# A four-layer graph attention stack on one core: the order of work planned for pairs of graphs, with tiles placed by colouring

## The chip, the core and the metric

The kernel runs on one core of a Trainium2 chip. The metric is the device time of one execution in microseconds (us). Before the change the median of three runs is 3231.36 us (3228.59 to 3233.77). The engines are named as in the profile: PE (matrix products), PEld (loading of the stationary operand for PE), DVE (vector), ACT (scalar functions), POOL (general vector), SP (issues most of the DMAs). Each engine works through its own queue in order, and semaphores hold an instruction until what it needs is there.

## What is computed

128 independent graphs of 128 nodes with 512 features each pass through four attention layers. Each layer is followed by a residual sum and a layer norm. Cut to what matters:

```
# layer 0: one head, scores from x itself
a = softmax(where(adj + eye == 0, -inf, leaky(s_src[:,None] + s_dst[None,:] + b)))
x = layernorm(x + a @ x)
# layer 1: two nested layers, 4 heads of 256, then 1 head of 512; softmax over the sources
xl = x @ W1                       # 512 -> 1024, plus 8 score columns
h  = elu(attention(xl) + b1)
x  = layernorm(x + attention(h @ W2) + b2)      # 1024 -> 512, plus 2 score columns
# layer 2: 8 heads of 64
h  = x @ W                        # 512 -> 512, plus score columns
x  = layernorm(x + concat(attention_per_head(h)))
# layer 3: one head, scores from x, elu of the result
x  = layernorm(x + elu(attention(x)))
```

All of it is in float32. A matmul of float32 operands is two records of PE in the profile (the mask transpose is one).

## The kernel before

One graph is a list of some 180 operations, each with an engine, a cost, an `emit` function, and the tiles it reads and writes. The list is made by `graph` (L567), in three parts:

- `first` (L830): loads, masks, layer 0, the norm, and the turning of x for the first projection. `project` (L704, matmuls at L710, evictions at L717) then makes the first projection, four chunks of four matmuls of 258 columns.
- `second` (L864): attention with four heads; the attention product and the bias and elu (`block`, L896 on PE, L902 on ACT, L903 on DVE). The elu is made as min(exp(v), 1) and max with the sum in PSUM; it is written into a tile of its own beside the tile of exponentials.
- `third` (L911): attention of the nested second layer, norm (L681 to L699), the last projection (L710 with wha), eight heads in two groups of four (`heads`, L938 and L942), the norm, and layer 3 (wide attention products at L725).

`attend` (L637) is the common attention step: ACT's Prelu per head (L646), DVE's masking with a running minimum (L654), ACT's exponential per head (L663), DVE's reciprocal (L671). `turned` (L602) transposes in two steps: DVE turns blocks of 32 (L607), the tile is written to DRAM (scr, L612) and is read back in another order (L617 or L622). `spread` (L580) lays a column of scores over all partitions, also by way of DRAM (row, L592 and L596). Each graph issues 30 DMAs from SP's queue.

The second projection (1024 to 512) is made for two graphs at a time with a seven-product scheme of Strassen's kind (`halves`, L749): POOL makes four sums of the left operands (L780), PE seven products of four matmuls of 257 columns (L794) in four PSUM banks, and evictions go by ACT (L807) or by a DVE addition (L812). As the list is per graph, a pair's products are divided between the list of the odd graph and that of the next even one.

The order of work is set by a planner that runs while the program is built (`Pipeline`, L75). `plan` (L79) places one graph's operations on every engine in a period of 28 us, by costs and by delays between engines that stand in a table. `order` (L145) then runs the operations of all graphs as a list: each engine takes the ready operation that can start first, at most 20 us ahead of the oldest one that is not issued. It counts 4.5 us and a shared lane for a DMA. A tile is given a place when it is first written, and the place is the one that has been free longest:

```
                b.slot = free[b.tag].pop(0)[1]
```

The places of each kind are as many as the plan needs; PSUM has eight. The setup of the weights (L305 to L555) is in the same list, with times of its own.

Of the kernel before, what the change touches and what calls it, by code (L numbers as in the profile page):

```python
# [26 lines left out]

PERIOD = 28.0
LATENCY = {"PE": (0.0, 0.8), "DVE": (0.15, 1.44), "ACT": (0.1, 1.44), "POOL": (0.1, 1.44), "SP": (7.06, 7.06)}
FLOW = {"PE": (0.0, 0.6), "DVE": (0.15, 0.8), "ACT": (0.1, 0.8), "POOL": (0.1, 0.8), "SP": (4.5, 4.5)}
AHEAD = 20.0
URGENCY = 0.6
BANKS = 8

SEED, SPREAD = 989, 8.0


class Buf:


    def __init__(self, tag, shape, dtype=F32):
        self.tag, self.shape, self.dtype = tag, shape, dtype
        self.size = 1
        for d in shape[1:]:
            self.size *= d

        if dtype is F32 and shape[0] == P and self.size in (P, 4 * P, 8 * P) and not tag.startswith(("ps", "scr")):  # L50
            self.tag = f"w{self.size}"
        self.ap = self.slot = None

# [7 lines left out]
class Op:  # L61
    def __init__(self, engine, cost, emit, ins, outs, extra, uses=(), dma=0.0):
        self.dma = dma
        self.engine, self.cost, self.emit, self.extra = engine, cost, emit, extra
        self.wait = 0
        self.ins, self.outs = ins, outs
        self.uses = list(uses)
        self.bufs = list(dict.fromkeys([*ins, *outs, *uses]))

    def done(self, reader=None):  # L70
        own, other = LATENCY[self.engine]
        return self.cost + self.extra + (own if reader is self.engine else other)


class Pipeline:  # L75
    def __init__(self, make, n, place):
        self.make, self.n, self.place = make, n, place

    def plan(self, ops):  # L79


        before, after = [set() for _ in ops], [[] for _ in ops]
        last, readers = {}, {}
        for k, op in enumerate(ops):
            for b in op.ins:
                before[k].add(last[b])
            for b in op.outs:
                if b in last:
                    before[k].add(last[b])
                before[k].update(readers.get(b, ()))  # L90
            before[k].discard(k)
            for q in before[k]:
                after[q].append(k)
            for b in op.ins:
                readers.setdefault(b, set()).add(k)
            for b in op.outs:
                last[b], readers[b] = k, set()
        left = [0.0] * len(ops)
        for k in reversed(range(len(ops))):
            left[k] = ops[k].cost + max(  # L100
                (left[q] + ops[k].done(ops[q].engine) - ops[k].cost for q in after[k]), default=0.0
            )
        taken = {e: [] for e in LATENCY}
        times, ready, missing = [0.0] * len(ops), [0.0] * len(ops), [len(q) for q in before]
        waiting = [k for k in range(len(ops)) if not missing[k]]
        rng = random.Random(SEED)
        shift = [SPREAD * rng.random() for _ in ops]
        while waiting:
            k = min(waiting, key=lambda k: (ready[k] - URGENCY * left[k] + shift[k], k))
            waiting.remove(k)  # L110
            op, t = ops[k], ready[k]
            spans = taken[op.engine]
            while True:
                u = t % PERIOD
                clash = [
                    y + d - u for x, y in spans for d in (-PERIOD, 0.0, PERIOD)
                    if u < y + d - 1e-9 and x + d < u + op.cost - 1e-9
                ]
                if not clash:
                    break  # L120
                t += min(clash) + 1e-9
                assert t < ready[k] + 2 * PERIOD, "the period is too short"
            spans.append((t % PERIOD, t % PERIOD + op.cost))
            times[k] = t
            for q in after[k]:
                ready[q] = max(ready[q], t + op.done(ops[q].engine) + max(ops[q].wait, 0) * PERIOD)
                missing[q] -= 1
                if not missing[q]:
                    waiting.append(q)
        return times  # L130

    def run(self, setup):
        times, events = self.plan(self.make(None)), [(t, -1, k, op) for k, (t, op) in enumerate(setup)]
        for g in range(self.n):
            for k, op in enumerate(self.make(g)):
                if op is not None:
                    events.append((g * PERIOD + times[k], g, k, op))
        events.sort(key=lambda e: e[:3])
        for g, op in self.order(events):
            for b in op.outs:  # L140
                if b.ap is None and b.slot is not None:
                    b.ap = self.place(b, g)
            op.emit()

    def order(self, events):  # L145

        ops, n = [e[3] for e in events], len(events)
        ends, first, last, readers, open_uses = {}, {}, {}, {}, {}
        before, after = [0] * n, [[] for _ in ops]
        makes, coming = [[] for _ in ops], {}  # L150
        for i, op in enumerate(ops):
            need = {last[b] for b in op.ins + op.uses if b in last}
            for b in op.outs:
                need.update([last[b]] if b in last else [], readers.get(b, ()))
                if b not in first:
                    first[b] = events[i][0]
                    if b.tag != "const":
                        makes[i].append(b)
                        coming.setdefault(b.tag, []).append(i)
            need.discard(i)  # L160
            before[i] = len(need)
            for q in need:
                after[q].append(i)
            for b in op.ins + op.uses:
                readers.setdefault(b, []).append(i)
            for b in op.outs:
                last[b], readers[b] = i, []
            for b in op.bufs:
                open_uses[b] = open_uses.get(b, 0) + 1
                ends[b] = max(ends.get(b, 0.0), events[i][0] + op.done())  # L170

        free = {}
        for b, t in first.items():
            if b.tag != "const":
                places = free.setdefault(b.tag, [])
                s = next((s for s, e in enumerate(places) if e <= t), len(places))
                places[s : s + 1] = [ends[b]]
        assert len(free["ps"]) <= BANKS, "too few banks"
        free = {tag: [(0.0, s) for s in range(BANKS if tag == "ps" else len(p))] for tag, p in free.items()}
        ready, released, clock, lane = [0.0] * n, {}, {e: 0.0 for e in FLOW}, 0.0  # L180
        known = {e: [i for i in range(n) if not before[i] and ops[i].engine == e] for e in FLOW}
        issued, low, out = [False] * n, 0, []

        def start(i):
            t = max(clock[ops[i].engine], ready[i])
            for b in makes[i]:

                rank = 0
                for q in coming[b.tag]:
                    if q >= i or rank >= len(free[b.tag]):  # L190
                        break
                    rank += 1
                if rank >= len(free[b.tag]):
                    return None
                t = max(t, free[b.tag][rank][0])
            return t

        while len(out) < n:
            best = None
            for e, waiting in known.items():  # L200
                found = None
                for i in waiting:
                    if events[i][0] > events[low][0] + AHEAD and i != low:
                        break
                    t = start(i)
                    if t is not None and (found is None or t < found[0]):
                        found = (t, i)
                        if t <= clock[e]:
                            break
                if found and (best is None or found < best):  # L210
                    best = found
            t, i = best
            op = ops[i]
            known[op.engine].remove(i)
            issued[i] = True
# [6 lines left out]
            if op.engine == "POOL":  # L222
                other += op.extra
# [20 lines left out]
def tile_gat_stack(  # L244
# [86 lines left out]
    def spread_row(t, r, a):  # L331
# [5 lines left out]
        return b  # L337

# [700 lines left out]
```

## Time and profile before

| what | value |
|---|---|
| median of three runs | 3231.36 us |
| profiled execution: its span | 3258.4 us |
| instructions in it | 62058 |
| PE busy | 94% of the span |
| DVE, ACT, POOL busy | 85%, 75%, 58% |
| granted PE clock, mean | 0.976 |
| DMA | 606.08 MB, 186 GB/s |

The profiled execution is one execution of its own. Its time is its span, from the first to the last instruction of the program, and it is 27.0 us longer than the median of the runs.

The page first gives each engine's busy time and its share of the span. A strip of 40 digits then shows that share in tenths, slice by slice. Groups of instructions are named by line, engine, operation and tile, with the idle time of the engine before them and what ended it. Matmuls overlap, and their ends are modelled, so a PE that is shown busy may still lose time between two starts.

### The profile page before, as it was taken

How to read it: one execution, taken by the hardware profiler on the slowest of the kernel's cores; microseconds unless marked ns; L12 is line 12 of the kernel's file. 1: busy time of each engine (PE TensorE's matmuls, PEld its weight loads, DVE VectorE, ACT ScalarE, POOL GpSimd, SP SyncE). 2: the span in 40 equal slices, each digit the busy share in tenths (PEclk: the TensorE clock that was granted, in tenths of full speed). 3: DMA queues.
4: the chain of work that ended last, by engine and by line, in shares of the span. 5: the costliest groups of instructions: out<-in, count | busy, mean ns of one | idle time of the engine just before them, and what ended most of it. 6: DMA issues, size and time to landing. Idle time of an engine off the chain costs nothing. (4 is left out here: it accounts for less than half of the span.)

```text
span 3258.4 us, 62058 instructions
## 1 busy us (share of the span) xinstructions
PE 3066.8 (94%) x14822; PEld 2488.7 (76%) x14822; DVE 2779.0 (85%) x9833; ACT 2451.2 (75%) x8741; POOL 1895.1 (58%) x2347
## 2 busy tenths in 40 slices
PE   6899999999999999999999999999999999999984
PEld 4688887787777877877777778777787777878853
DVE  4779888888888988898888889889898898989875
ACT  2457787787777777787777877777877777778875
POOL 4655655665565655665555665565566556565533
PEclk7899999999999999999999999999999999999985
DMA  4358777877877877877778777877787787777875
GB/s 119 94 136 196 183 205 188 200 193 190 203 187 188 205 186 192 201 190 200 188 187 200 191 188 204 189 190 201 191 204 187 188 205 188 196 196 190 197 174 129
DMA packets 1657567, 606.08 MB, mean 186 GB/s; under 512 B 1311562, under 2 KB 1508170, under 8 KB 1657204
## 3 DMA queue, kind: packets, MB, share of 16 engines
q1 hardware_dynamic: 1655836, 598.97, 75.0%
q8 instruction: 120, 1.97, 0.2%
q14 instruction: 243, 1.99, 0.2%
q0 software_dynamic: 576, 2.10, 0.2%
q10 hardware_dynamic: 792, 1.06, 0.1%
HBM read 374.43 MB, written 227.48 MB: 185 GB/s over the span
## 5 line engine op out<-in xcount | busy, mean ns | idle before, releaser
L710 PE MATMUL ps<-w1s,w 128*128 128x258 f32 x4096 | 926.9, 384 | 48.5 <-DMA w<-scr 25.0
L710 PEld LDWEIGHTS ps<-w1s,w 128*128 128x128 f32 x4096 | 777.0, 191 | 186.3 <-DVE xl L812 39.5
L654 DVE CUSTOM_DVE_ANT_0 w<-w,w 128x128 f32<-128x128 f32 x1920 | 861.1, 544 | 65.6 <-ACT w L646 49.2
L794 PE MATMUL ps<-w2s,w 128*128 128x257 f32 x3584 | 849.0, 383 | 8.5 <-POOL w L780 8.4
L663 ACT ACTIVATE w<-w,nm 128x128 f32<-128x128 f32 x1920 | 748.0, 394 | 98.2 <-DVE nm L654 76.3
L794 PEld LDWEIGHTS ps<-w2s,w 128*128 128x128 f32 x3584 | 669.1, 191 | 188.8 <-issue 80.0
L646 ACT ACTIVATE w<-w,xl 128x128 f32<-128x128 f32 x1536 | 488.8, 389 | 279.9 <-DMA w<-row 259.1
L607 DVE STREAM_TRANSPOSE w<-w 128x512 f32<-128x512 f32 (+1 forms) x1024 | 551.5, 540 | 34.3 <-ACT w L663 13.3
L710 PE MATMUL ps<-wha,w 128*128 128x273 f32 x2048 | 502.3, 398 | 7.3 <-DMA w<-scr 6.9
L710 PEld LDWEIGHTS ps<-wha,w 128*128 128x128 f32 x2048 | 383.2, 192 | 87.4 <-DVE w L607 6.3
L699 ACT ACTIVATE w<-w,mr,rd 128x512 f32<-128x512 f32 x512 | 415.2, 811 | 33.9 <-POOL mr L692 33.0
L692 POOL TENSOR_SCALAR mr<-mv,rd 128x1 f32<-128x1 f32 x512 | 160.1, 313 | 409.4 <-ACT rd L686 201.8
L663 ACT ACTIVATION_READ_ACCUMULATOR w<-w,nm 128x1 f32 x1920 | 368.1, 192 | 0.0
L681 DVE BATCH_NORM_STATS2 st<-w 128x6 f32<-128x512 f32 x512 | 337.2, 668 | 5.4 <-POOL w L986 4.6
L881 POOL TENSOR_TENSOR xl<-xl,b1t 128x512 f32<-128x512 f32 x256 | 335.2, 1310 | 1.6
L938 PEld LDWEIGHTS ps<-xl,w 128*128 128x128 f32 x2048 | 274.3, 196 | 80.8 <-issue 24.4
L646 ACT ACTIVATE w<-w,sc 128x128 f32<-128x128 f32 x384 | 152.3, 397 | 227.6 <-DMA w<-row 226.6
L725 PE MATMUL ps<-w,w 128*128 128x512 f32 x512 | 277.4, 624 | 32.6 <-DMA w<-scr 31.6
L738 POOL TENSOR_SCALAR w<-adj 128x128 f32<-128x128 int32 x256 | 192.4, 752 | 188.2 <-DMA adj<-in_adj_dram 75.1
L717 ACT COPY xl<-ps 128x258 f32<-128x258 f32 (+1 forms) x768 | 273.2, 362 | 31.8 <-PE ps L710 31.3
L938 PE MATMUL ps<-xl,w 128*128 128x66 f32 x2048 | 265.2, 273 | 27.7 <-DMA w<-scr 14.4
L654 DVE DVE_READ_ACCUMULATOR2_ANT nm<- 128x1 f32 x1920 | 290.5, 151 | 0.0
(213 smaller groups left out, 4258.8 us busy)
## 6 DMA issues: line engine op xcount, KB each, us to landing
scr<-w SPq DMA_DIRECT2D x640, 256.0 KB
w<-scr SPq DMA_DIRECT2D x640, 256.0 KB
w<-row SPq DMA_DIRECT2D x128, 512.0 KB
w<-in_x_dram SPq DMA_DIRECT2D x128, 256.0 KB
w<-row SPq DMA_DIRECT2D x128, 256.0 KB
out_dram<-w SPq DMA_DIRECT2D x128, 256.0 KB
w<-row SPq DMA_DIRECT2D x384, 64.0 KB
scr<-w SPq DMA_DIRECT2D x384, 64.0 KB
```

The lines of the kernel that those rows point to most:

```text
L607: op("DVE", 0.12 + 0.133 * n, lambda: nc.vector.transpose(zb.ap.rearrange("p b h c -> p h b c"), src.ap.rearrange("p (h b c) -> p h b c", ...
L646: nc.scalar.activation(z.ap[:, h, :], db.ap[:, h0 + h, :], AF.Prelu, bias=src(h0 + h), alpha=SLOPE)
L654: nc.vector.tensor_tensor_reduce(out=zz.ap[:, h, :].rearrange("p (b a) -> p a b", b=4), in0=z.ap[:, h, :].rearrange("p (a b) -> p a b", b= ...
L663: nc.scalar.activation(zz.ap[:, h, :], zz.ap[:, h, :], AF.Exp, bias=nm.ap[:, h : h + 1], scale=-1.0, accum_out=rs.ap[:, h : h + 1],)
L681: op("DVE", 0.6, lambda: nc.vector.bn_stats(st.ap, y.ap), [y], [st])
L699: op("ACT", 0.7, lambda: nc.scalar.activation(y.ap, y.ap, AF.Identity, bias=mr.ap, scale=rd.ap), [y, rd, mr], [y])
L710: op("PE", w * 4 / 2400 + 0.006, lambda k=k: nc.tensor.matmul(px.ap[:, :w], lhsT=lhs.ap[:, k, :], rhs=wa(k, c), start=(k == 0), stop=(k == ...
L717: op("ACT", 0.06 + w / 1200, lambda: nc.scalar.copy(dst(), px.ap[:, :w]), [px], [t])
L725: op("PE", width * 4 / 2400, lambda: nc.tensor.matmul(pa.ap[:, :width] if len(xv.shape) == 2 else pa.ap.rearrange("p (s c) -> p s c", s=2) ...
L794: return lambda: nc.tensor.matmul(q[b].ap[:, :C2], lhsT=x()[:, k, :], rhs=w2s[:, slot, k, :], start=(fresh and k == 0), stop=(k == 3), ski ...
L881: op("POOL", 1.3, lambda nh=nh: nc.gpsimd.tensor_add(xl.ap[:, nh, : 2 * FH], xl.ap[:, nh, : 2 * FH], b1t[:, nh * 2 * FH : (nh + 1) * 2 * F ...
L938: op("PE", 0.225, lambda u=u, h=h: nc.tensor.matmul(pa.ap[:, u * CH : (u + 1) * CH], lhsT=pt.ap[:, u, :], rhs=xl3.ap[:, h * CH : (h + 1) * ...
```

## The change

The list is now made for a pair of graphs (`pair`), with one list of operations per pair and the two graphs' first parts half a period apart. Strassen's products stand in it as one unit. The planner is three functions: `needs` finds the dependences, `plan` places one pair in a period of 53 us, and `lay_out` runs all pairs as a list, at most 60 us ahead. An operation has a duration for each of its parts, as the profile shows them, and each engine a tail. A DMA takes 1.7 us to start, its time on a lane that all share, and 0.6 us to land, with at most eight under way. POOL and those DVE operations that are marked `port` exclude one another. Evictions into one tile are `joins`: they are not ordered among themselves. All matmuls of an accumulation are one operation. Places are given after the list run, by colouring: a tile takes, among the places that the run left free early enough, the one freed last.

```diff
-PERIOD = 28.0
-LATENCY = {"PE": (0.0, 0.8), "DVE": (0.15, 1.44), "ACT": (0.1, 1.44), "POOL": (0.1, 1.44), "SP": (7.06, 7.06)}
-FLOW = {"PE": (0.0, 0.6), "DVE": (0.15, 0.8), "ACT": (0.1, 0.8), "POOL": (0.1, 0.8), "SP": (4.5, 4.5)}
-AHEAD = 20.0
...
-SEED, SPREAD = 989, 8.0
+PERIOD, PACE, AHEAD = 53, 53, 60
+HOP = {'PE': 0.5, 'DVE': 0.5, 'ACT': 0.5, 'POOL': 0.5, 'SP': 1.0}
+URGENCY, SEED, SPREAD = 0.3, 87533, 16.0
+BANKS, PRODUCTS = 8, 2
...
+FLIGHT, LANDS = 1.7, 0.6
+LANES = 8
+SLACK = 1.0
...
+        if e == "POOL":
+            u = max(u, vector_until)
...
+            if op.port:
+                u = max(u, pool_until)
...
+        if e == "SP":
+            lane = max(lane, t + FLIGHT) + op.dma
+            got = [lane + LANDS]
...
+    for b in sorted({b: None for op in ops for b in op.bufs if b.tag != "const"}, key=lambda b: b.began):
+        places = free.setdefault(b.tag, [])
+        slack = 0.0 if b.tag in scarce else SLACK
+        fit = [s for s in range(len(places)) if places[s] + slack <= b.began]
+        b.slot = max(fit, key=lambda s: places[s]) if fit else len(places)
+        places[b.slot : b.slot + 1] = [b.until]
```

Strassen's scheme uses three banks. Bank pa holds four of the products one after another, adding up, and is evicted between them; the last one needs no addition on DVE:

```diff
+        product(pa, left[0][0], 0, True)
...
+        taken(pa, t1)
+        product(pc, left[0][1], 1, True)
+        added(pc, t1, 0, 0)
+        product(pa, s[1], 4, False)
+        product(pb, s[0], 3, True)
+        taken(pa, u2)
+        taken(pb, v)
+        product(pa, s[2], 5, False)
+        product(pb, s[3], 2, False)
+        added(pa, v, 1, 1)
+        added(pb, u2, 0, 1)
+        product(pa, left[1][1], 6, False)
+        copied(pa, wide, lambda: to(1, 0), joins=[out[1]])
```

The elu is made in place, and each half of its result is a tile of its own:

```diff
-                op("ACT", 0.6, lambda: nc.scalar.activation(half(e1), pa.ap, AF.Exp, bias=minus[:, 0:1]), [pa], [e1])
-                op("DVE", 0.65, lambda: nc.vector.scalar_tensor_tensor(
-                    out=half(hT), in0=half(e1), scalar=1.0, in1=pa.ap, op0=ALU.min, op1=ALU.max
-                ), [e1, pa], [hT])
+            op("ACT", 0.585, lambda pa=pa, whole=whole: nc.scalar.activation(whole(), pa.ap, AF.Exp, bias=minus[:, 0:1]), [pa], [hT[c]])
+            op("DVE", 0.585, lambda pa=pa, whole=whole: nc.vector.scalar_tensor_tensor(
+                out=whole(), in0=whole(), scalar=1.0, in1=pa.ap, op0=ALU.min, op1=ALU.max
+            ), [hT[c], pa], [hT[c]])
```

The setup's work for the second and the last projection is the same, and its times in the list are earlier (for the sums of the second projection's weights 50 to 71 instead of 89 to 109, for the last projection's columns 79 to 113 instead of 139 to 201). In the new program the first projection, the second and the last one share one matmul line (L702), the evictions are at L710, the attention products at L838 (first layer), L878 (heads) and L771 (wide), and Strassen's additions at L747.

## The prediction

> **What bounds the kernel now.** I read the page's first two parts, then the table of stretches, then who waited for whom in the even middle, 400 to 2900 us.
>
> ```profile
> PE 3066.8 (94%) x14822; PEld 2488.7 (76%) x14822; DVE 2779.0 (85%) x9833; ACT 2451.2 (75%) x8741; POOL 1895.1 (58%) x2347
> PE   6899999999999999999999999999999999999984
> PEclk7899999999999999999999999999999999999985
> ```
>
> PE is busy in nine slices of ten, and only the first and last slices are weak, in its share and in its granted clock. So there are three stages: fill, middle, drain.
>
> ```profile
> 58.00:134.00 76.00, 60.85 (x244) 47.00 (x244) 55.67 (x129) 34.60 (x111) 63.20 (x59) 0.81 0.39 98
> ...
> 400.00:2900.00 2500.00, 2413.65 (x11882) 1973.60 (x11882) 2201.57 (x7856) 1956.23 (x7025) 1495.68 (x1859) 1.00 0.79 194
> 2900.00:3069.00 169.00, 164.55 (x819) 136.09 (x818) 147.47 (x532) 135.72 (x489) 99.84 (x126) 1.00 0.80 197
> 3069.00:3259.00 190.00, 130.26 (x522) 96.26 (x521) 131.19 (x486) 131.13 (x452) 68.11 (x103) 0.75 0.65 155
> ```
>
> Columns: stretch, its length, then busy us of PE, PEld, DVE, ACT and POOL, granted clock, DMA share, GB/s. In the middle PE is busy 2413.65 of 2500 us. L896 has 1648 matmul records there and 16 in a graph, so 103 graphs pass: 24.27 us each, 0.84 us of it with PE idle. What PE must spend I take from starts in its timeline, from the start of a run to that of the next: first projection 6.96, first-layer attention 1.79, last projection 3.69, heads twice 0.83, wide attention products three times 0.86, second projection 14 x 0.44, mask transpose 0.14, in all 22.98 us. So 1.29 us of a graph is loss: 0.84 shows as idle, 0.45 is hidden between starts. No other engine is above 88% (DVE 2201.57 of 2500) and DMA is at 0.79: **PE bounds it**, and a reordering can win at most what PE loses.
>
> ```profile
> PE ps L710 <- DMA w<-scr: 22.9, 23, 1.7
> PE ps L725 <- DMA w<-scr: 14.7, 25, 1.3
> PE ps L850 <- DVE w L903: 13.7, 14, 1.9
> PE ps L710 <- DVE ri L671: 9.3, 9, 2.1
> ...
> PEld ps L710 <- DVE xl L812: 36.9, 29, 2.5
> ...
> PEld ps L725 <- ACT xl L717: 26.2, 46, 1.7
> ```
>
> Waits of matmuls and, below the dots, of weight loads in the middle: us in total, times, longest. 37.6 us of PE's 86 idle us is for data that comes by way of DRAM (w<-scr). The weight loads' waits on L812 and L717, which are evictions of PSUM, are waits for a bank: 1.27 and 0.57 us each.
>
> **The change, part by part.** It removes no matmul and no DMA. In the built programs PE has 7475 matmuls before and after, ACT 6820 instructions, POOL 2349, SP 3873 DMAs; DVE has 64 fewer. So the sum is about order and waits.
>
> *Three-bank Strassen.* One DVE addition in each pair of graphs becomes a plain ACT eviction (there were four of L807 and there are three and one of its kind now). 64 x 404 ns (L812) = 26 us of DVE go. DVE is idle 12% of the middle: nothing on the path. Bank pa now takes four products in a row; each needs the eviction of the one before. In the built order even the closest two of one bank have 1.88 us of other PE work between them (a product and a transpose), against L812's 0.40 us and an eviction's 0.36. I cost it at 0; if DVE comes late there, a wait is 1.27 us as for L812 today.
>
> *elu in place, the two halves of hT as separate buffers, evictions of one tile unordered among themselves.* Same instructions (L902, L903, L981, L982). Cost 0; their order on one queue was kept anyway. Matmuls of a chain issued together instead of singly: same start-to-start times expected, 0.
>
> *Setup.* The same loads and products; those of the second and last projection are due some 40 to 90 us earlier. They are POOL's (16 of 1.25 us from L472, 16 of 1.2 us from L504), and POOL is busy 63 of 76 us from 58 to 134 us. PE's work ahead of the first projection is 13.5 us against 15.3. I take 0, from -15 (the weak fill has 39 us of PE idle) to +10 (one mask late: PE's L850 once waited 9.0 us for L738).
>
> *Drain.* After the last matmul of the first projection 301 DVE operations are left in the old order and 242 in the new (SP 177 and 143), and 99.9 and 74.9 us of PE work. The drain lasts 190 us now. By operations left it would be 190 x 242/301 = 153, so -37; the 25.0 us of PE work now done earlier cost 25.0 x 24.27/22.98 = +26. Sum **-11**; between -37 (the moved work fits into idle time) and 0.
>
> *The list run.* Its own durations now agree with rows: a masked softmax step 0.226 (L654 starts 0.23 apart), wide transposes 0.61, an exponential 0.387 (0.29 and its accumulator read). It also gives each DMA a queue of eight and a time by size, holds POOL and some DVE operations apart, and gives small tiles more places (nm4 five for one, rs4 four for one). From 134 to 3069 us some 121 graphs' worth of time passes. Ends: none of the idle goes (0), or all of it (121 x 0.84 = -102). I take half, nearest to the share that is waits for DMA (37.6 of 86 us), the thing that the new durations describe better: 121 x 0.42 = **-51**.
>
> *Places by colouring, for the banks too.* The old order took the bank that had been free longest, the new one takes the one freed last. Counted in the built order with the durations above, the PE work between a bank's last matmul and its next tenant falls from a median of 7.4 us to 1.8; in 16% of the takings, five in a pair, it is under 1 us, where formerly none was under 2. An eviction needs 0.36 us (L717) and some hand-over. This adds waits on ACT and DVE behind which all of PE stands, and every engine behind PE. No row has such a wait at such a distance; the nearest is L725 on L717, 0.57 us each. Ends: never (0), or half of the five and a quarter of the eleven others under 2 us, 5.2 a pair: 64 x 5.2 x 0.57 = +190. I take one in two pairs, **+18**: the run itself knew each bank to be free at that time.
>
> Here the trace comes first: L725's 46 waits on L717 show that late evictions do stop PE. The Trainium skill, "Perfetto Trace Analysis", section "Matmuls", says that independent groups should rotate through different PSUM banks so that one's evacuation overlaps the next; it speaks against this colouring. It gives no price; by it the sum would take the upper end, 3231 - 62 + 190 = 3359, by the rarity of such waits in the rows it stays at 3187.
>
> Another row: POOL's one-column L692 waited 123.9 us for L654, which writes nothing it reads. The Trainium skill, "SBUF — State Buffer", section "SBUF: two separate sides", calls the port pair of DVE and GpSimd an exclusive lock held for a whole instruction. By the rule 15 masks of 0.23 us would lock POOL out 3.4 us a graph; the row has 123.9/103 = 1.2 us. POOL is at 60%, so neither moves the sum.
>
> *Sum.* -11 - 51 + 18 = -44 us on the profiled span of 3258.4, which is 3214. That execution is 27 us above the median of 3231.36, so the median goes to 3231.4 - 44 = **3187 us**.
>
> **Rivals.** *A. Banks bind: slower.* Place: PE's first matmul or weight load of a group, held by the eviction of the group just before. For it: the distances above, ACT idle for 420 us of the middle behind late row broadcasts (L646 on w<-row, 281 times, up to 3.8 us), with evictions queued behind them. Against it: the run planned for it, and a stalled PE gives the next eviction more time. Price 0.57 us a wait; it decides from 62/(64 x 0.57) = 1.7 waits a pair, where it eats the other two terms. At three to four a pair: 64 x 3.5 x 0.57 = 128, less 62: 3297 us.
>
> *B. The first projection comes late: slower.* From the first attention product to that projection the old order has 24.5 us of PE work, the new one 13.6 for odd graphs and 17.6 for even. The bare chain is L733, L681, L682, L685, L686, L692, L699, L607 (0.73+0.67+0.16+0.29+0.20+0.31+0.81+0.54 = 3.7), two issues (1.1) and two DMAs (3.86 for w<-scr in the chain that ended last, taken for both): 12.5 us; 13.6 x 24.27/22.98 = 14.4 are there. If the queues add 4 us, PE waits 2.1 us a pair, 134 in all, less 62: 3303. Against it: the plan puts this chain first, and with 24.5 us the old one filled its time with waiting.
>
> *C. A trade: no change to speak of.* Old waits go and new ones come; only the drain is shorter, 3231 - 11 = 3220, within a band of 3205 to 3240.
>
> *D. PE nearly full.* All idle goes and the drain gives 11: 3231 - 113 = 3118. For it: PE alone is over 90% used, and a dozen graphs in flight leave it a choice.
>
> **How the numbers follow.** Forecast (3187, between 3140 and 3205) 0.35, A 0.28, B 0.10, C 0.17, D 0.10. Both signs are likely, so the range reaches from D's middle to A's: 3115 to 3310, leaving out under a fifth (A with five waits a pair, B with more lateness). The forecast's own range is 3140 to 3205. A measurement of this kernel tells 0.2% from no change. Faster by over that: 0.35 + 0.10 + half of C = 0.53; same 0.08; slower 0.39.
>
> **What would show it.** In the middle of the new profile, PE idle under 0.5 us a graph and a graph in under 23.9 us: the list run is right. Waits of PE on the copies that `copied` makes (L710) or on exponentials that read PSUM, more than two a pair: A. PE's L702 on w1s behind DMA w<-scr at over 1 us a pair: B. Time from the last first projection to the end under 180 us: the drain. DVE busy down by 26 us: the addition. I would be wrong altogether if start-to-start times of matmuls changed, or the granted clock in the middle fell below 1.00.

## The result, and the profile after

The changed kernel takes 3466.16 us in the median (3461.63 to 3477.45, four runs). On the same chip the kernel before takes 3229.98. The ratio is **1.0757, 95% interval 1.0723 to 1.079**: slower by 7.6%, outside the range that was forecast. The profiled execution has a span of 3475.6 us, 217.2 more than the one of before.

The page's first two parts, to be laid beside those of before:

```profile
PE 3155.8 (91%) x14822; PEld 2496.6 (72%) x14822; DVE 2885.5 (83%) x9769; ACT 2501.8 (72%) x8741; POOL 1887.4 (54%) x2347
...
PE   5898999999999999999999999999999999899984
...
PEclk9899999999999999999999999999999999999995
```

The work is the same by its counts, except for the 64 DVE additions that went. Every engine's share of the span fell, PE's from 94% to 91%. In a kernel that PE bounded this means that no single engine bounds it now: the engines wait for each other. The strips show no single bad stage; the loss is spread over the run.

The table of stretches, middle only (columns as above):

```profile
400.00:2900.00 2500.00, 2333.10 (x11135) 1857.54 (x11133) 2150.43 (x7303) 1875.56 (x6576) 1402.73 (x1747) 0.99 0.74 181
```

The attention product, now L838, has 1552 records there, so 97 graphs pass instead of 103 (by whole graphs, so to about 1%): 25.77 us each instead of 24.27. PE idles 1.72 us a graph instead of 0.84; the rest of the 1.50 us is hidden between starts. From start to start inside a run the projections' matmuls take what they took before (median 217 to 230 ns by shape, the same within 1 ns). DVE's busy time is 22.17 us a graph (2150.43/97) where it was 21.37, ACT's 19.34 (18.99), POOL's 14.46 (14.52): nothing that comes near 25.77.

Now the waits of matmuls and, below the dots, of weight loads in the same stretch:

```profile
PE ps L702 <- DVE w L846: 46.2, 40, 2.3
PE ps L702 <- ACT u L710: 19.8, 22, 2.0
PE ps L702 <- ACT xl L710: 18.4, 28, 3.1
PE ps L771 <- ACT xl L710: 14.3, 25, 1.7
...
PE ps L702 <- DMA w<-scr: 6.3, 8, 2.5
...
PEld ps L702 <- DVE w L846: 70.6, 59, 2.6
PEld ps L702 <- ACT xl L710: 50.4, 78, 3.3
PEld ps L771 <- ACT xl L710: 46.0, 65, 1.8
```

L710 is the eviction in `copied`, L846 the elu in place, which is the last reader of a bank and also makes operands of the second projection. DMA, first among the waits of before, is down to 6.3 us. Matmuls wait on L710 in six groups of 74.0 us and 105 times together, 2.2 a pair of graphs, and weight loads 136.1 us besides. This is the picture that rival A described. The experiments say that it misleads.

SP's own queue shows one more thing, before and then after: how long it stood at a read-back from DRAM (w<-scr) until the write ahead of it (scr<-w) had landed.

```profile
SPq L622 <- DMA scr<-w: 17.5, 22, 2.4
SPq L617 <- DMA scr<-w: 7.5, 12, 1.5
...
SPq L631 <- DMA scr<-w: 144.0, 131, 3.4
```

25.0 us became 144.0. The order now issues such a read before its data are there, and the DMAs behind it in SP's queue stand with it.

Last, the chain that ended last, by engine and by line, for the whole program:

```profile
DVE 26%; PE 23%; DMA 20%; ACT 15%; issue 6%; POOL 3%; SPq 3%; DVEq 0%; POOLq 0%; ACTq 0%
PE ps L702 17%; DMA w<-row 14%; DVE w L650 8%; ACT w L645 6%; DVE w L617 4%; DVE st L676 3%; ACT w L659 3%; ACT w L693 3%; DMA w<-scr 3%; PE ps L878 2%; DVE w L846 2%; DVE w L779 2%; PE ps L771 2%; DMA scr<-w 2%; PE ps L838 1%
```

PE has only 23% of it. The rest goes through the masked softmax (L650), exponentials (L645, L659), turning (L617) and the row broadcast by DMA. The chain before could be followed only at its end, so its shares are not to be set against these; but a chain with PE in under a quarter of it is not that of a PE that is fully used.

### The profile page after: what moved, and what is told of

It is laid out like the page before. It is cut to its first block, busy times and chain, and to the rows that moved or that the text cites. A ratio compares the mean times of both kernels' runs of the same rounds, so it can differ in the third digit from the quotient of the medians.

```text
span 3475.6 us, 62183 instructions
## 1 busy us (share of the span) xinstructions
PE 3155.8 (91%) x14822; PEld 2496.6 (72%) x14822; DVE 2885.5 (83%) x9769; ACT 2501.8 (72%) x8741; POOL 1887.4 (54%) x2347
## 4 chain that ended last, share of the span: by engine, by line
DVE 26%; PE 23%; DMA 20%; ACT 15%; issue 6%; POOL 3%; SPq 3%; DVEq 0%; POOLq 0%; ACTq 0%
PE ps L702 17%; DMA w<-row 14%; DVE w L650 8%; ACT w L645 6%; DVE w L617 4%; DVE st L676 3%; ACT w L659 3%; ACT w L693 3%; DMA w<-scr 3%; PE ps L878 2%; DVE w L846 2%; DVE w L779 2%; PE ps L771 2%; DMA scr<-w 2%; PE ps L838 1%
## 5 line engine op out<-in xcount | busy, mean ns | idle before, releaser
L702 PE MATMUL ps<-w1s,w 128*128 128x258 f32 x4096 | 967.3, 387 | 52.9 <-DMA w<-scr 21.9
L702 PE MATMUL ps<-w2s,w 128*128 128x257 f32 x3584 | 863.5, 392 | 92.9 <-DVE w L846 52.1
L702 PEld LDWEIGHTS ps<-w1s,w 128*128 128x128 f32 x4096 | 771.4, 192 | 244.3 <-ACT xl L710 60.2
L650 DVE CUSTOM_DVE_ANT_0 w<-w,w 128x128 f32<-128x128 f32 x1920 | 837.4, 529 | 89.6 <-ACT w L645 86.6
L702 PEld LDWEIGHTS ps<-w2s,w 128*128 128x128 f32 x3584 | 688.3, 196 | 231.9 <-DVE w L846 67.7
L659 ACT ACTIVATE w<-w,nm 128x128 f32<-128x128 f32 x1920 | 747.6, 392 | 129.4 <-DVE nm L650 118.7
L617 DVE STREAM_TRANSPOSE w<-w 128x512 f32<-128x512 f32 (+1 forms) x1024 | 543.0, 540 | 92.5 <-ACT w L693 41.8
L645 ACT ACTIVATE w<-w,xl 128x128 f32<-128x128 f32 x1536 | 485.4, 391 | 169.3 <-DMA w<-row 154.5
L702 PE MATMUL ps<-wha,w 128*128 128x273 f32 x2048 | 512.8, 397 | 14.5 <-DVE w L846 6.5
L702 PEld LDWEIGHTS ps<-wha,w 128*128 128x128 f32 x2048 | 378.4, 190 | 140.9 <-DVE w L846 22.2
L710 ACT COPY xl<-ps 128x258 f32<-128x258 f32 (+2 forms) x832 | 301.9, 365 | 210.7 <-PE ps L702 207.9
L659 ACT ACTIVATION_READ_ACCUMULATOR w<-w,nm 128x1 f32 x1920 | 364.4, 190 | 0.0
L725 POOL TENSOR_TENSOR w<-w,w 128x512 f32<-128x512 f32 x256 | 325.6, 1282 | 47.3 <-DVE w L846 19.8
L669 POOL TENSOR_TENSOR w<-w,ri 128x512 f32<-128x512 f32 (+1 forms) x256 | 201.4, 796 | 260.4 <-DVE ri L667 153.5
L838 PEld LDWEIGHTS ps<-w,xl 128*128 128x128 f32 x2048 | 250.5, 194 | 93.7 <-issue 39.4
L771 PE MATMUL ps<-w,w 128*128 128x512 f32 x512 | 276.7, 624 | 36.1 <-DMA w<-scr 21.8
L838 PE MATMUL ps<-w,xl 128*128 128x128 f32 x2048 | 263.2, 281 | 41.6 <-DMA w<-scr 16.2
L878 PEld LDWEIGHTS ps<-xl,w 128*128 128x128 f32 x2048 | 262.9, 195 | 53.0 <-ACT xl L710 22.6
```

Of the source, the lines that this page charges most:

```text
L617: op("DVE", {1: 0.215, 4: 0.61}[n], lambda: nc.vector.transpose(zb.ap.rearrange("p b h c -> p h b c"), src.ap.rearrange("p (h b c) -> p h ...
L645: nc.scalar.activation(zh(h), db.ap[:, h0 + h, :], AF.Prelu, bias=src(h0 + h), alpha=SLOPE)
L650: nc.vector.tensor_tensor_reduce(out=zz.ap[:, h, :].rearrange("p (b a) -> p a b", b=4), in0=zh(h).rearrange("p (a b) -> p a b", b=4), in1= ...
L659: nc.scalar.activation(zz.ap[:, h, :], zz.ap[:, h, :], AF.Exp, bias=nm.ap[:, h : h + 1], scale=-1.0, accum_out=rs.ap[:, h : h + 1],)
L702: nc.tensor.matmul(px.ap[:, :w], lhsT=lhs(k), rhs=rhs(k), start=(fresh and k == 0), stop=(k == nk - 1), skip_group_check=True,)
L725: op("POOL", cost, lambda: nc.gpsimd.tensor_tensor(out=own[o][1](), in0=a[1](), in1=b[1](), op=what), [a[0], b[0]], [s[o]])
```

## The theories

1. **Banks.** A PSUM tile takes the bank freed last, a late eviction holds up the next chain, and PE stands (rival A).
2. **Hand-offs counted without margin.** The run of the list decides the order by when it believes each result to be there. The kernel before counts 0.6 us from PE, 0.8 from the others and 4.5 for a DMA. The change counts 0.06 and a tail of 0.05 to 0.165, so 0.11 to 0.23 us, and 1.7 + 0.6 and its size on the lane for a DMA. With queues served in order, an operation that comes later than believed holds up all that stands behind it on its engine.

Three more came up on the way: that the places in SBUF and DRAM bind, for which the same line of code decides (theory 3), that the plan starts a pair's operations too late, with too little work in flight (theory 4), and that the pair as the unit, with both graphs and Strassen's products in step, costs by itself (theory 5).

## The experiments

Ratios are to the kernel before, run beside on the same chip; its median was 3254 to 3259 us there.

**e1, banks only.** In the giving of places:

```diff
-        places = free.setdefault(b.tag, [])
+        places = free.setdefault(b.tag, [0.0] * BANKS if b.tag == "ps" else [])
...
-        b.slot = max(fit, key=lambda s: places[s]) if fit else len(places)
+        b.slot = (min if b.tag == "ps" else max)(fit, key=lambda s: places[s]) if fit else len(places)
```

> The changed kernel with one edit: a PSUM tile takes the bank that has been free longest, out of all eight, instead of the one freed last; the order of work is untouched. Theory 1 (banks): in the changed kernel's trace PE waits 1.37 us a graph for a bank (133 us of the 2500 between 400 and 2900 us), against 0.24 before. These go: a graph falls from 25.77 to 24.3-24.7 us, the time to 3290-3340 us. Theory 2 (the order itself: durations without a margin): the stalls move to data, the time stays above 3420 us. Theory 3 (places in SBUF): also above 3420 us.

Measured: 3495.14 us, **1.0743 (1.0712 to 1.0773)**, the same as the changed kernel. Its waits of matmuls in the middle:

```profile
PE ps L702 <- DMA w<-scr: 45.6, 24, 4.4
PE ps L702 <- DVE w L846: 43.6, 38, 2.7
PE ps L702 <- ACT u L710: 22.0, 16, 3.3
PE ps L702 <- DVE xl L747: 18.8, 9, 3.1
PE ps L702 <- DVE nm L650: 14.5, 8, 3.6
```

The waits of matmuls on L710 of xl are all but gone, as the edit intended (1.2 us are left), and in their place stand waits for data: w<-scr up from 6.3 to 45.6 us, the masking (L650) new. PE stands no less than it did (idle 190.9 us of the 2500, 166.9 in after), for something else. A wait that has the largest sum need not be what costs the time: take it away, and the next late thing is waited for. One thing blurs the size: the granted clock of e1's runs was 0.954 to 0.960, that of after 0.971 to 0.977. If PE bound, that would cost e1 some 56 us (an estimate: 0.016 of 3495), so a gain of up to 1.6% from the banks could be hidden here; the 3290 to 3340 us that theory 1 expected could not. Theory 1 falls as the cause of the loss.

**e2, the other places.** `min` and `max` are exchanged in that last line, so SBUF and DRAM tiles take the longest free place and banks the last freed.

> The changed kernel with the other half of that edit: every tile in SBUF and DRAM takes the place that has been free longest among those the colouring has, the banks stay as they are. Theory 3 (places in SBUF tie the engines together): below 3400 us. Theory 1 (banks) and theory 2 (order): within 25 us of 3466.

Measured: 3496.08 us, **1.0744 (1.0715 to 1.0773)**: nothing.

**e3, all places longest free**: `min` for every kind, with all eight banks from the start as in e1.

> Both edits. Theory 1: as the run with banks alone, 3290-3340 us, within 20 us of it. Theory 3: clearly below that run, by 40 us or more. Theory 2: above 3420 us.

Measured: 3489.85 us, **1.0716 (1.0681 to 1.0751)**. That is 0.4 points less than the changed kernel for both together, with intervals that overlap.

**e4, the other way round: the kernel before with banks freed last.** As its order is made along with its places, the order changes too.

```diff
-                b.slot = free[b.tag].pop(0)[1]
+                spots = free[b.tag]
+                last = max((j for j, s in enumerate(spots) if s[0] <= t), default=0) if b.tag == "ps" else 0
+                b.slot = spots.pop(last)[1]
```

> The kernel before with one edit: a PSUM tile takes the bank freed last among those free at that time. Theory 1: its graphs become slower in the same way, bank waits rise from 0.24 to about 1 us a graph: 3310-3380 us. Theory 2 or 3: within 25 us of 3230.

Measured: 3279.08 us, **1.0077 (1.0054 to 1.01)**. Banks freed last do cost the kernel before something, a tenth of what is to be explained.

**e5, margin between engines only.**

```diff
-SEES = {"PE": 0.06, "DVE": 0.06, "ACT": 0.06, "POOL": 0.06, "SP": 0.0}
+SEES = {"PE": 0.45, "DVE": 0.65, "ACT": 0.65, "POOL": 0.65, "SP": 0.0}
```

With the tails this makes 0.6 us from PE and 0.7 to 0.75 from the others, near what the kernel before counts.

> The changed kernel, whose list run counts 0.06 us from an engine's end (with its tail 0.11 to 0.23 us) until another engine sees it; here it counts 0.5 us more for a hand-off between engines, so about the 0.6 to 0.8 us that the order before counted. Only the order and the places change. Theory 2 (an order without margin: a late operation holds up all that stands behind it in its engine's queue): faster than the changed kernel, 3466 to below 3400 us if the engines' hand-offs are what lacks margin. Theory 4 (the work moved less far ahead: fewer graphs in flight): no gain, within 30 us of 3480, or slower.

Measured: 3433.84 us, **1.0539 (1.0509 to 1.0569)**. Two points come back from one line of constants. The time lies between what theory 2 (below 3400 us) and theory 4 (within 30 us of 3480) expected, on a chip where the kernel before takes 3258.68.

**e8, the margin taken from the kernel before.**

```diff
-FLOW = {"PE": (0.0, 0.6), "DVE": (0.15, 0.8), "ACT": (0.1, 0.8), "POOL": (0.1, 0.8), "SP": (4.5, 4.5)}
+FLOW = {"PE": (0.0, 0.23), "DVE": (0.15, 0.15), "ACT": (0.1, 0.16), "POOL": (0.1, 0.11), "SP": (2.3, 2.3)}
```

> The kernel before, with the changed kernel's hand-offs in its list run: 0.23, 0.15, 0.16 and 0.11 us after PE, DVE, ACT and POOL instead of 0.6 to 0.8, and 2.3 us for a DMA instead of 4.5. The units stay graphs, four banks, the place free longest. Theory 2: the kernel before becomes slower as the change did, by 4% or more, above 3360 us. Theory 5: within 1.5% of before.

Measured: 3350.33 us, **1.0296 (1.0268 to 1.0323)**. Its matmuls' waits in the middle:

```profile
PE ps L794 <- ACT u L807: 71.0, 31, 4.7
PE ps L710 <- ACT xl L717: 33.9, 36, 2.9
PE ps L794 <- POOL w L986: 13.9, 6, 3.1
```

That is slower by 3.0%, between the 4% or more of theory 2 and the 1.5% of theory 5, so most of the 7.6% does not follow from these counts alone in the old kernel. Nothing else of the change is in it: its banks are given longest free, and its Strassen scheme has four of them. And yet its matmuls now wait 71.0 us on L807, which is not in before's list, and 33.9 on L717, on which they wait 3.8 there. So an order without margin can show itself as waits on evictions; a likely way is that an eviction behind something late on ACT's queue is itself late. In this kernel the same counts also say when a bank is free again, so that its margin went with the others. The list of waits of after could not tell the two theories apart. SP's wait for landed writes came with the smaller counts here too: L622 on scr<-w is 163.2 us, 17.5 before.

**e6b, margin for DMAs only.** Every DMA counts 4.5 us and its size. With the spare time of 1.0 us before a place is used again, the tiles of this order would take 147.2 KB of a partition (143.6 with the margin of e5 as well) and 142.4 are there, so the spare time is 0 in this kernel and in those that have this margin below.

```diff
-FLIGHT, LANDS = 1.7, 0.6
-LANES = 8
-SLACK = 1.0
+FLIGHT, LANDS = 1.7, 2.8
+LANES = 12
+SLACK = 0.0
```

> The changed kernel, whose list run counts 4.5 us and a time by size for a DMA instead of 2.3 us (FLIGHT 1.7, LANDS 2.8, twelve under way); the colouring's slack is 0 instead of 1 us, so that the tiles fit in SBUF. The margin between engines, added alone, brought the ratio to before from 1.076 to 1.054. Theory 2 (an order without margin), if DMAs matter too: 1.03 to 1.05 (3360 to 3420 us). If only the engines' hand-offs matter: 1.065 or more.

Measured: 3506.01 us, **1.0772 (1.0756 to 1.0788)**: alone, nothing. Yet it did what it was meant to do. SP's wait for landed writes and the largest wait of matmuls in the middle:

```profile
SPq L631 <- DMA scr<-w: 5.2, 7, 1.7
...
PE ps L702 <- DVE w L779: 52.9, 29, 3.7
```

SP's wait fell from 144.0 to 5.2 us, and PE was idle 189.0 us all the same, now behind engines: L779 reads a bank on DVE.

**e7b, both margins**: the edits of e5 and e6b together, so one line (`SEES`) apart from e6b.

> Both margins (0.5 us more for a hand-off between engines, 2.2 us more for a DMA), slack 0. Theory 2: the two add up, ratio 1.00 to 1.03. Theory 5 (the pair as the unit, with both graphs and Strassen's products in step, costs by itself): stays above 1.04.

Measured: 3310.75 us, **1.0174 (1.0156 to 1.0192)**. From 1.0757 this is 5.8 points of 7.6, and from e6b 6.0 by the counts between engines alone. Theory 5, which asked for more than 1.04, falls. The middle, and the largest waits of matmuls in it:

```profile
400.00:2900.00 2500.00, 2409.43 (x11784) 1960.05 (x11783) 2257.34 (x7724) 1967.28 (x6953) 1488.59 (x1845) 1.00 0.79 192
```

```profile
PE ps L702 <- ACT xl L710: 19.5, 27, 1.9
PE ps L702 <- DVE w L779: 13.9, 17, 2.5
PE ps L838 <- ACT xl L710: 5.9, 7, 1.5
```

PE's busy time is back from 2333.10 to 2409.43 (before: 2413.65). The wait on L846, 46.2 us in after, is 3.7 here, and the one on u by L710 is no longer among the groups. What is left at the top are waits for banks: L710 on xl, and L779, which frees a bank too. A bank's release got no margin by these edits: the list run counts it free a tail and 0.05 us after its last reader, 0.14 to 0.15 us for DVE and ACT, where the kernel before counts 0.8.

**e9, more in flight.** The plan's hops are raised, so that it starts each pair's operations earlier against its later ones; the run of the list is as in the change.

```diff
-HOP = {'PE': 0.5, 'DVE': 0.5, 'ACT': 0.5, 'POOL': 0.5, 'SP': 1.0}
+HOP = {'PE': 0.8, 'DVE': 0.9, 'ACT': 0.9, 'POOL': 0.9, 'SP': 2.0}
```

> The changed kernel, with longer hand-offs in the plan of one pair alone (0.8 to 0.9 us instead of 0.5 between engines, 2.0 instead of 1.0 for a DMA); the list run counts as in the change. Due times of one graph's operations lie further apart, so more graphs are under way. Theory 4 (too little in flight): ratio below 1.055. Theory 2 (it is the list run's own counts): within 0.012 of 1.076.

Measured: 3513.47 us, **1.0801 (1.0776 to 1.0825)**. Theory 4, which asked for less than 1.055, falls: the same kind of margin gives nothing in the plan.

**e10, both margins and all places longest free**: e7b with the giving of places of e3.

> Both margins, and every place and bank the one free longest (eight banks). With the order as in the change this edit of the places did nothing (1.0716 against 1.0757). Theory 2 says the same here, within 0.01 of the run with both margins; theory 1 in a second form (places bind once the order is sound): lower than it by 0.015 or more.

Measured: 3243.73 us, **0.9961 (0.9946 to 0.9975)**: 0.4% faster than the kernel before. Its first part and its middle:

```profile
PE 3065.5 (95%) x14822; PEld 2506.2 (77%) x14822; DVE 2861.7 (88%) x9769; ACT 2464.0 (76%) x8741; POOL 1907.1 (59%) x2347
```

```profile
400.00:2900.00 2500.00, 2432.22 (x11957) 2004.94 (x11956) 2288.47 (x7838) 1982.44 (x7067) 1514.85 (x1872) 0.99 0.81 195
```

```profile
PE ps L702 <- DMA w<-scr: 13.4, 16, 3.0
PE ps L702 <- DVE w L846: 10.7, 10, 2.0
PE ps L771 <- DMA w<-scr: 9.7, 11, 3.0
```

PE is the most used engine again, at 95%, idle 0.65 us a graph, and waits first for data by way of DRAM, as before. The places that gave next to nothing in e1 to e3 now give 2.1 points: theory 1 in the second form that was expected for this run, where theory 2 had said no more than 1. The longest free place supplies slack that the counts for releases leave out; that this is how it works is argued, not shown.

**e11, which places.** e7b with the giving of places of e1, banks alone longest free.

> The changed kernel with both margins (between engines 0.45 from PE and 0.65 from the others, DMAs 4.5 us and their size) in its list run, and with the PSUM tile taking, of the eight banks, the one that has been free longest; the SBUF and DRAM tiles still take the place freed last. With both margins the ratio was 1.0174, with both margins and every place longest free 0.9961. If the banks make those 2.1 points (a late eviction holds up the next chain of matmuls), the ratio is 0.993 to 1.002. If the SBUF and DRAM places make them (a late reader of a tile holds up the DVE, ACT or DMA that writes the next one in its place), it stays at 1.013 to 1.02. In between, both do.

Measured: 3270.3 us, **1.0037 (1.0021 to 1.0053)**. Of the 2.1 points 1.4 are the banks' and 0.8 the other places', taken in this order; this is the "in between" of the expectation.

**e12, more margin still.** e10 with 0.9 instead of 0.65 us from DVE, ACT and POOL.

> The changed kernel with both margins and every place longest free (0.9961 before this), its hand-offs from DVE, ACT and POOL counted at 0.9 us instead of 0.65, from PE at 0.45 as before, DMAs as before. If the order still has too little margin (margin theory, with its optimum beyond what the kernel before had), the ratio falls below 0.993. If 0.65 is about enough, more margin only starts work earlier than needed and the ratio stays at 0.993 to 1.001. If every operation that is started early costs places and time, it is above 1.001.

Measured: 3291.53 us, **1.011 (1.0093 to 1.0128)**. More is not better: 0.9 costs 1.5 points against 0.65. On the other side, 0.06 costs 6.0 points (e6b against e7b, which have the same DMA margin and the same giving of places). The best value of those tried is the middle one; there were only these three.

## Why the prediction was wrong

Each profiled execution divided by the first and the last start of a first projection's matmul (ps<-w1s) shows where the terms stand. Times in us:

| kernel | until the first | first to last | last to end | span |
|---|---|---|---|---|
| before | 58.0 | 3010.6 | 189.8 | 3258.4 |
| after | 51.7 | 3268.8 | 155.1 | 3475.6 |
| e7b, both margins | 66.6 | 3066.5 | 175.5 | 3308.6 |
| e11, and banks | 58.1 | 3029.0 | 174.5 | 3261.6 |
| e10, and all places | 57.5 | 3010.2 | 174.2 | 3241.9 |
| e8, before without margin | 54.6 | 3111.3 | 182.9 | 3348.8 |

- **The list run, -51: the step that failed.** It was worked out from "its own durations now agree with rows", and half of PE's idle time was taken as the gain. The same lines of the diff cut what the run counts from one engine to another from 0.6 and 0.8 us to between 0.11 and 0.23, and for a DMA from 4.5 to 2.3 us and its size, and this was not priced at all; the ends, 0 and -102, held no loss, although a better-fitted duration excludes none. Measured, first to last grew by 258.2 us. Margins take 202.3 of it away (3268.8 to 3066.5), banks 37.5 more, other places 18.8, and there is then no gain left: 3010.2 against 3010.6. These are single executions on several chips, on which the kernel before differs by up to 29 us; by the ratios, which are free of that, the three are worth about 190, 45 and 25 us. So with margin and places kept, the step is worth about 0, and without the margin about +190 to +200.
- **Banks, +18.** The mechanism was seen and is there, but its size is 37.5 us once the order has margin (45 by the ratios), at least twice the term, and by itself nothing that e1 could show. The reason given for the small term, that the run itself knew each bank to be free, fails with the step above: the run knew it by counts without margin. The row comes first here: 46 waits of weight loads of the wide products (L725) on L717 before, 26.2 us, and 65 (L771) on L710 after, 46.0 us. Of matmuls themselves only 9 waited on L717, 3.8 us in all, so the row was weaker support for "stop PE" than it was taken for. The Trainium skill, "Perfetto Trace Analysis", section "Matmuls", asks for independent groups to rotate through different banks; by that the changed kernel should have gained from e1. It gained nothing to be seen (1.0743 against 1.0757), at a lower clock. In e11 the rule holds, with 1.4 points. So the rule was clearly worth something here only with an order that had its margin.
- **Rival A** had the right sign, and its mark in the trace (over two waits a pair) came true at 2.2. It was the wrong mechanism for the time all the same: e1 removed most of the mark (19 waits of matmuls of 23.2 us in all are left) and none of the time. A mark that other causes leave as well, as e8 shows, cannot decide.
- **Rival B** is refuted: L702 on w<-scr, over all projections, is 6.3 us in some 48 pairs, 0.13 us a pair where over 1 was its mark.
- **Drain, -11: right in sign, too small.** 189.8 to 155.1 us, -34.7, near the end of -37 that was given; the 25 us of PE work done earlier cost no visible time in a stretch that was not bound by PE. Where PE binds again (e10) it is -15.6, close to the term, and that is all that e10 gains.
- **Three-bank Strassen, 0.** DVE's additions (L812, now L747) fell from 103.3 to 80.0 us, near the 26 that was reckoned. In after the wait of products for the bank pa (L702 on u, L710) is 19.8 us in the middle, which had been put at 0; with both margins it is gone. DVE as a whole did not fall by 26 us, as the prediction's last part asked, but rose from 2779.0 to 2885.5 us. It is nearly as high in e10 (2861.7), which is faster than before, so this is not the loss; that mark asked too much of a page's total.
- **Setup, 0, and start-to-start times**: the first projection starts 6.3 us earlier, inside -15 to +10, and start-to-start times are unchanged, as expected.
- **Granted clock.** "I would be wrong altogether if ... the granted clock in the middle fell below 1.00" was said; it fell to 0.99. That 1% of matmul time could not make 7.6%.

**What is shown and what is argued.** Shown: the counts of the list run make most of the loss. With both margins 5.8 of the 7.6 points come back (e7b), 6.0 of them by the one line of the counts between engines when the DMA margin is there (e6b to e7b). Taken from the kernel before, the margins cost it 3.0 points (e8), the same way but not most. The places make the rest, and only with the margins: 0.4 points without them (e3), 2.1 with them (e10), while the margins give 5.8 points with the one giving of places and 7.6 with the other (e3 to e10). Argued: the way in which lateness spreads. Queues in order, SP's wait for landed writes, which comes and goes with the DMA margin, and a chain with PE in 23% of it speak for it, but no run followed a single late operation from queue to queue. **Open:** why DMA margin gives nothing alone (e6b, +0.15 points, intervals overlapping) and 3.7 points on top of e5. The rows say that waits for DMAs then turn into waits between engines; a loop that passes through engines and DMAs by turns would do that. e6b also changed the number of lanes and the spare time of places, which were not tried singly. Three-bank Strassen, elu in place and the measured durations were not tried by themselves either; e10 holds all three and is faster than before, so what they cost together is small there.

## What to carry to other kernels

In an order that is fixed before the run, a hand-off count is not an estimate to be made exact but a margin to be chosen: with the counts cut to 0.11 to 0.23 us the whole order ran late, here by 6%, and the largest waits of PE named another cause. When every engine's share falls and the chain of waits has no engine in most of it, look at the order and its margins before taking away the largest wait; and change a suspected wait for real before believing it, since the same edit of the banks gave nothing to be seen with one order and 1.4 points with another. In a diff of a planner, price each constant that it believes in, also those that are merely smaller.

## What the runs showed of the hardware

- **The granted clock differed and the time did not.** e1 and e2 ran on one chip and took the same time (3495.14 and 3496.08 us). The mean clock of the profiled executions was 0.954 in e1 and 0.978 in e2, their spans 3502.4 and 3490.3 us; the other runs of each lie near (0.959 to 0.960 and 0.974 to 0.975). The two give places differently, so it is not shown that the clock cost nothing: a gain from the banks may have covered it. Their middles, e1 and then e2, differ in the clock (third number from the end) and little in the rest:

```profile
400.00:2900.00 2500.00, 2309.15 (x11024) 1884.70 (x11023) 2112.19 (x7240) 1856.84 (x6525) 1383.47 (x1724) 0.97 0.73 180
```

```profile
400.00:2900.00 2500.00, 2307.16 (x11054) 1834.10 (x11052) 2130.70 (x7257) 1862.38 (x6536) 1390.36 (x1732) 1.00 0.74 180
```

- **DMAs through scr landed sooner in the slower kernel.** From issue to the semaphore of the landing, between 250 and 3000 us, the median of scr<-w is 2.88 us in after and 3.85 in before (all sizes), that of the commonest shape of w<-scr (256 KB) 3.87 and 4.32, and that of w<-row (all sizes) much the same, 3.89 and 3.93. So the loss is not one of slower transfers. The DMA share in the middle was lower too (0.74 against 0.79).
- **The kernel before, unchanged, differed by 0.9% from place to place** (medians of 3229.98 us beside the changed kernel, 3254.6 to 3258.68 on the chips of the experiments), more than the 0.2% that is told apart beside it on one chip. Only ratios to a kernel run beside on the same chip can be compared.
